# Key and query weights loaded behind the branch, layer 3's output read first, and unread products on TensorE

## The chip, the cores and the metric

The kernel runs on one core of one Trainium2 chip. The metric is the device time of one execution in microseconds, and the figure given is the median of several runs. The engines of a core work side by side, each through its own queue in order: TensorE (PE: matrix products, with a separate record for loading weights), VectorE (DVE), ScalarE (ACT) and GpSimd (POOL). SyncE (SP) issues the transfers between DRAM and on-chip memory; they run on 16 DMA engines.

## What is computed

Input x is 32 images of 1024 channels and 14 x 14 positions. Two residual layers follow one another, each behind a group normalisation:

```
x = x + conv(_gn(x))         # three convolutions as table look-ups
x = x + attention(_gn(x))    # linear attention
```

In the first layer each convolution is a softmax over 16 centroids for each group of inputs, multiplied by a table, with a batch normalisation over all images behind it; the third one's output is added to the layer's input. The second layer is

```
q = elu(Wq x[:, :512] + bq) + 1 ;  k = elu(Wk x[:, 512:] + bk) + 1
z = 1 / (q . mean(k) + 1e-6)
kv = rope(k) x^T / n ;  attn = (rope(q) kv) * z
out = attn + depthwise3x3(x)
```

for 16 heads of 64 channels. All is in float32.

## The kernel before, in words

`layers` runs the three convolutions over the images. Its last stage computes the third convolution in 14 chunks of 448 tokens: 8 products for each of 8 channel tiles (L1005), a copy out of PSUM on ACT (L1013), statistics on DVE (L1014), and one store of the chunk, 1792 KB, to the DRAM buffer `o3d` (L1022). `bn_final` then makes scale and bias of the batch normalisation (`sc3`, `bi3`, L325 to L329).

The exponentials are taken without subtracting a maximum; whether all sums stayed in range is collected in a small number, `again`. After `layers` stands a branch, `tc.If(again > 0)` (L1036), which runs everything once more in a slower, safe form if needed. With this data it is skipped. Every engine executes the jump. At the end of the branch SP waits on each of the semaphores of its eight outstanding DMAs, and the other engines wait for SP.

Eight tiles of 128 x 1024 values, `weights` (named `lut0` to `lut7`), hold the tables of the convolutions in turn and later the weights of keys (`wk`, the first four) and queries (`wq`, the last four). `attention_inputs` returns the pieces that prepare the attention while the convolutions still run: small tables, x of the first pair of images (`x1`, `x0`, by halves of the channels), and the second half of the third convolution's output for the first pair (`o3_0`, `o3_1`). Its function `projections` issues the eight loads of the weights, 512 KB each. Before the change it is called after `layers`, ahead of the branch (`weights4(None)`), and again in the branch (`repeated`), where the tables overwrite the tiles.

Behind the branch `tb = gn_b + bi3` is made on DVE (L1061), some borders are cleared on POOL, and then 16 pairs of images go through a plan. `do(engine, rank, weight, fn, reads, writes, ...)` enters a piece with its engine, a due time (`rank`, lower is earlier), an estimated duration, and the keys that it reads and writes. `Plan.write` then plays the pieces through with the estimates: whenever an engine is free it takes the ready piece of the lowest rank whose buffers (`Slot`, taken from rings of tiles) are to be had. The order so found is the order of the instructions in each engine's queue. What an instruction waits for on the chip follows from the tiles that it touches, not from the plan's keys.

For a pair p and a half h (h = 1 are channels 512 to 1023, from which the keys come, and it goes first), the pieces that matter here are:

- `load`: SP loads x (for p > 0) and two tiles `o` of 392 KB with the third convolution's output from `o3d` (L1172). The ring `o3q` for these has no tiles of its own; it gets `o3_0` and `o3_1` once the first pair's half h = 1 has read them. So the reads for half h = 0 of the first pair wait for DVE.
- `front`: for each of four channel tiles ACT scales x into PSUM (L1192), DVE adds `o` times `sc3` (L1201), adds x (L1206), and takes statistics (L1211).
- `group_norm`: PE averages over groups with a matrix `gavg` (L1233), DVE centres (L1241 to L1246), PE averages squares, DVE adds epsilon (`gve`, L1249), POOL makes scale and shift (`ga`, `gb`).
- `normalise`: ACT writes the normalised `y` (L1286) and the scaled `x` for the depthwise convolution's middle tap (L1286 too).
- `channels`: PE multiplies `y` by a column block of `wk` or `wq` (L1318, four products of 392 columns), ACT takes relu (L1327) and exp (L1330), DVE takes the maximum (L1335 or L1339).
- `rope`, `tokens`, `products`, `normalisers`, `attend`, `lepe`: rotation on POOL, transposes on PE with copies on ACT (L1380, L1383), products of keys and values (L1417), denominators, attention (L1522) and the depthwise taps on DVE (L1540).

PSUM has four tiles `mm` for these products, three `pa` and one `w`. The ring `qr` has five tiles of 128 x 784 values, for rotated queries.

## Time and profile before

| | us |
|---|---|
| three runs | 3863.39, 3867.28, 3868.2 |
| median | 3867.28 |
| the profiled execution | 3861.88 |
| its span, first to last instruction | 3860.0 |
| PE busy | 3715.2 |
| DVE busy | 3002.4 |
| POOL busy | 2300.7 |
| ACT busy | 1687.7 |

All times below are counted from the start of the span of the profiled execution. The convolutions take until about 2662 us, the last store of `o3d` is issued at 2661.92, the plan's first instruction runs at 2682.18, and the first key product starts at 2703.04. In the record of PE a product in float32 appears as two matrix products. "Busy" of PE is the time covered by products, and their ends are modelled; the granted clock (PEclk) is a share of the full clock. The instructions that wait, branch or issue a DMA stand under the engine's queue, such as SPq.

### The profile page before, as it was taken

Reading aid. Unit: us, or ns where it says so; the run is one execution under the profiler, and the core shown is the slowest. Engines: PE = TensorE matmul, PEld = TensorE weight load, DVE = VectorE, ACT = ScalarE, POOL = GpSimd, SP = SyncE. Lnnn points to the kernel's source line nnn. Section 1 sums busy time; section 2 is a strip of 40 time slices with the busy share of each in tenths; the row PEclk is TensorE's granted clock in tenths of the full one; section 3 lists DMA queues with packets and bytes.
Section 4 is the critical chain, followed back from the end, with each engine's and each line's share of the span. In section 5 each row is a group of like instructions: output and inputs, shape, how many; then the busy total and the mean of one; then the engine's idle time right before and its main releaser. Section 6 shows DMA issues by size and latency. Waiting matters only on the chain. (4 is left out here: it accounts for less than half of the span.)

```text
span 3860.0 us, 45872 instructions
## 1 busy us (share of the span) xinstructions
PE 3715.2 (96%) x16415; PEld 2079.6 (54%) x16415; DVE 3002.4 (78%) x4281; ACT 1687.7 (44%) x3851; POOL 2300.7 (60%) x1338
## 2 busy tenths in 40 slices
PE   8999999999999999999999999995999999999998
PEld 5555555554555545555444444442666666666665
DVE  8999999978888888888633333332699999999996
ACT  4555555533333323333221222111766776666664
POOL 7999999974444444444311111110887888878886
PEclk9999999999999999999999999997999999999999
DMA  3111100015343333333111111103123223222221
GB/s 116 34 35 34 34 25 26 17 54 125 71 85 79 76 74 81 81 74 70 44 47 38 38 38 38 38 20 124 36 78 89 78 84 91 82 82 84 82 80 34
DMA packets 219107, 243.16 MB, mean 63 GB/s; under 512 B 24368, under 2 KB 216752, under 8 KB 218872
## 3 DMA queue, kind: packets, MB, share of 16 engines
q1 hardware_dynamic: 218296, 240.02, 23.3%
q8 instruction: 131, 2.15, 0.2%
q14 instruction: 104, 0.85, 0.1%
q10 hardware_dynamic: 576, 0.15, 0.0%
HBM read 163.55 MB, written 76.56 MB: 62 GB/s over the span
## 5 line engine op out<-in xcount | busy, mean ns | idle before, releaser
L596 POOL TENSOR_TENSOR t<-t,r 128x1664 f32<-128x1664 f32 (+1 forms) x284 | 1063.9, 3746 | 1188.3 <-DVE r L595 1153.8
L640 PE MATMUL po<-t,lut 128*128 128x392 f32 x4096 | 1418.1, 500 | 0.5 <-POOL t L596 0.5
L640 PEld LDWEIGHTS po<-t,lut 128*128 128x128 f32 x4096 | 759.9, 190 | 626.7 <-issue 123.7
L558 ACT ACTIVATE t<-sc,cbias 128x392 f32<-128x392 f32 (+1 forms) x1136 | 578.9, 592 | 1032.1 <-PE sc L906 646.6
L1318 PE MATMUL mm<-y,lut 128*128 128x392 f32 x2048 | 721.7, 500 | 4.8 <-DVE q L1335 2.9
L1005 PE MATMUL po<-t,lut 128*128 128x448 f32 x1792 | 682.2, 541 | 1.7 <-issue 1.7
L570 DVE STREAM_TRANSPOSE tt<-t 128x1664 f32<-128x1664 f32 (+1 forms) x284 | 544.3, 1917 | 167.8 <-ACT t L558 167.8
L595 DVE STREAM_TRANSPOSE r<-rc 128x1664 f32<-128x1664 f32 (+1 forms) x284 | 546.6, 1925 | 21.3 <-DVE rc L589 0.9
L1540 DVE SCALAR_TENSOR_TENSOR pa<-y,lepe_w,pa 128x406 f32<-128x406 f32 x900 | 540.7, 636 | 17.9 <-PE pa L1522 15.1
L1005 PEld LDWEIGHTS po<-t,lut 128*128 128x128 f32 x1792 | 339.0, 190 | 341.7 <-issue 341.5
L1318 PEld LDWEIGHTS mm<-y,lut 128*128 128x128 f32 x2048 | 375.7, 191 | 257.6 <-issue 14.3
L1014 DVE BATCH_NORM_STATS2 stats<-o 128x6 f32<-128x448 f32 x112 | 68.9, 617 | 487.5 <-ACT o L1013 487.5
L587 DVE TENSOR_REDUCE sm<-tt 128x104 f32<-128x832 f32 (+2 forms) x284 | 423.0, 1490 | 5.4
L573 POOL TENSOR_TENSOR tt<-tt 128x832 f32<-128x832 f32 x128 | 247.4, 1933 | 7.8 <-DVE tt L570 7.8
L1013 ACT COPY o<-po 128x448 f32<-128x448 f32 x112 | 59.0, 527 | 425.6 <-PE po L1005 381.2
L589 DVE RECIPROCAL rc<-sm 128x104 f32<-128x104 f32 (+1 forms) x284 | 229.5, 808 | 9.8
L897 PE MATMUL sc<-patch,cw 64*128 64x392 f32 x1024 | 210.4, 519 | 4.6 <-ACT t L558 2.5
L597 ACT ACTIVATE sm<-sm 128x104 f32<-128x104 f32 (+1 forms) x284 | 86.0, 303 | 177.1 <-DVE rc L589 176.9
L1503 POOL TENSOR_TENSOR qr<-qr,zb 128x784 f32<-128x784 f32 x64 | 117.6, 1850 | 70.2 <-DMA zb<-zd 68.2
L897 PEld LDWEIGHTS sc<-patch,cw 64*128 64x128 f32 x1024 | 90.5, 186 | 115.8 <-issue 74.2
L1327 ACT ACTIVATE e<-mm,kbd 128x392 f32<-128x392 f32 x128 | 74.1, 579 | 170.4 <-PE mm L1318 168.4
L1192 ACT ACTIVATE w<-x,tb,gn_a 128x196 f32<-128x196 f32 x248 | 128.2, 517 | 44.2 <-DVE tb L1061 20.9
(175 smaller groups left out, 3975.6 us busy)
## 6 DMA issues: line engine op xcount, KB each, us to landing
patch<-h1d SPq DMA_DIRECT2D x248, 162.8 KB
x<-in_x_dram SPq DMA_DIRECT2D x32, 784.0 KB
o3d<-o SPq DMA_DIRECT2D x14, 1792.0 KB
x<-in_x_dram SPq DMA_DIRECT2D x64, 392.0 KB
o<-o3d SPq DMA_DIRECT2D x64, 392.0 KB
out_dram<-x SPq DMA_DIRECT2D x64, 392.0 KB
h1d<-pad SPq DMA_DIRECT2D x96, 225.0 KB
patch<-h1d SPq DMA_DIRECT2D x124, 108.5 KB
```

Source lines behind the costliest of these rows:

```text
L558: nc.scalar.activation(t[:, j, : sc.shape[1]], sc, AF.Identity if exact else AF.Exp, bias=bias[:, j : j + 1],)
L570: nc.vector.transpose(tt, tf)
L573: nc.gpsimd.tensor_tensor(tv[:, :, :8], tv[:, :, :8], tv[:, :, 8:], ALU.add)
L587: nc.vector.tensor_reduce(sm, tv, AX.X, ALU.add)
L589: nc.vector.reciprocal(rc, sm)
L595: nc.vector.transpose(r, bc(rc, 2, KC))
L596: nc.gpsimd.tensor_tensor(tf, tf, r, ALU.mult)
L640: nc.tensor.matmul(po[h], luts[b][:, j, h * P : (h + 1) * P], ts[u % len(ts)][:, j, :N2], start=(b == 0 and j == 0), stop=(b == 7 and j == 3),
L897: nc.tensor.matmul(sc, w8[r, 8 * h + 4 * (j // 2) + g], grid(pbuf[n % NPB][r, j // 2, g]), start=True, stop=False,)
L1005: nc.tensor.matmul(po, luts[g][:, m * P : (m + 1) * P], t3[h][:, g % 4, :], start=(g == 0), stop=(g == 7),)
L1318: nc.tensor.matmul(pv(), w[kt][:, m0 : m0 + P], ywin(p, first + kt), start=(kt == 0), stop=(kt == 3),)
L1540: nc.vector.scalar_tensor_tensor(acc, neighbours(p, c, offset(k)), lw[:, c, k : k + 1], acc, ALU.mult, ALU.add,)
```

## The change

Four edits.

The loads of the weights become eight separate functions, one for each tile. They are no longer called ahead of the branch, nor in it; the plan enters them on SP with ranks of -90 to -83, the key weights first, and each writes a key `("w", b)` that the products of keys or queries read. The branch has no load of the weights ahead of it any more.

The two reads of the third convolution's output for the first pair's half h = 0 go into two tiles of the ring `qr` instead of `o3q`, and get a rank of -99. So SP's queue after the branch begins with two reads of `o3d` into `qr`, four loads of `wk`, four of `wq`, and then x of the second pair; before, it began with x of three halves, and then the reads of `o3d`.

Two pieces of PE work are added, of 16 and of 10 products of the identity with `tb`, 256 columns each, with a rank of -50. Nobody reads their results. The second piece names the key of `gve` of the first half as one that it reads, so the plan puts it behind the second average of that half; the tiles that it touches do not make it wait for `gve` on the chip. In PE's queue 16 products come first, then the two averages of half h = 1, the ten products, the two averages of h = 0, and the first keys.

The plan is played through anew with these pieces, and its order in the later pairs comes out different in places; which instructions there are does not change.

```diff
-        def projections(_):
-            for b in range(8):
-                t = a["wkT" if b < 4 else "wqT"]
-                load_lut(b, t[(b % 4) * P : (b % 4 + 1) * P])
-
-        return [loads, third, tables], projections, [third, projections]
+        def projection(b):
+            t = a["wkT" if b < 4 else "wqT"]
+            return lambda: load_lut(b, t[(b % 4) * P : (b % 4 + 1) * P])
+
+        return [loads, third, tables], [projection(b) for b in range(8)], [third]
...
         again = layers(False, early)
-        weights4(None)
...
-                ot = Slot("o3q")
+                ot = Slot("qr" if p == 0 and h == 0 else "o3q")
...
-                    do(SP, rank - 11 + 8 * k, 0.45, third, (), [(ot, 0), (ot, 1)], lag=4.5)
+                    r = rank - 11 + 8 * k if p > 0 else -99
+                    do(SP, r, 0.45, third, (), [(ot, 0), (ot, 1)], lag=4.5)
...
+        def warm(n, need):
+            pw = Slot("mm")
+
+            def piece():
+                for _ in range(n):
+                    nc.tensor.matmul(
+                        pw()[:, : CT * B],
+                        ident,
+                        tb.rearrange("p c b -> p (c b)"),
+                        start=True,
+                        stop=True,
+                    )
+
+            do(PE, -50, 0.4 * n, piece, need, [pw])
...
             do(DVE, rank, 0.1, variance, [pv], [key("gve")])
+            if p == 0 and h == 1:
+
+                for n, need in ((16, []), (10, [key("gve")])):
+                    warm(n, need)
...
+            need = [("w", b) for b in (range(4) if keys else range(4, 8))]
+
...
-            do(PE, rank, 2.76, product, ys_ + done, [pq, *held], lag=0.25)
+            do(PE, rank, 2.76, product, ys_ + done + need, [pq, *held], lag=0.25)
...
+        for b in range(8):
+            do(SP, b - 90, 0.95, weights4[b], (), [("w", b)], lag=3.5 + b)
         for p in range(NP):
             pair(p, T * p)
```

## The prediction

> **What bounds the kernel now.** I read the page's busy slices first: TensorE (PE) is busy in nine tenths of nearly every slice, except one with 5 tenths and a granted clock of 0.7, the 28th, at about 2605 to 2702 us. That is where layer 3 of the convolution hands over to the attention plan. I then cut that stretch into windows (columns: length, busy time of each engine with its instruction count, granted PE clock, DMA share, GB/s).

> ```profile
> 2661.00:2664.00 3.00, 0.33 (x1) 0.00 (x0) 1.33 (x3) 0.53 (x1) 0.59 (x1) 0.97 0.30 112
> 2664.00:2668.00 4.00, 0.00 (x0) 0.00 (x0) 0.50 (x3) 0.00 (x0) 1.06 (x1) 0.50 1.03 342
> 2668.00:2672.00 4.00, 0.00 (x0) 0.00 (x0) 0.00 (x0) 0.00 (x0) 0.00 (x0) 0.50 1.01 353
> 2672.00:2679.00 7.00, 0.00 (x0) 0.00 (x0) 0.00 (x0) 0.00 (x0) 0.00 (x0) 0.50 1.02 412
> 2679.00:2682.00 3.00, 0.00 (x0) 0.00 (x0) 0.00 (x0) 0.00 (x0) 0.00 (x0) 0.50 0.08 29
> 2682.00:2690.00 8.00, 0.00 (x0) 0.00 (x0) 6.32 (x15) 6.77 (x14) 2.83 (x14) 0.50 0.87 264
> 2690.00:2703.00 13.00, 3.87 (x16) 3.62 (x17) 8.31 (x29) 5.81 (x13) 2.62 (x6) 0.50 0.45 147
> 2703.00:2708.00 5.00, 5.00 (x9) 2.79 (x10) 1.99 (x5) 2.47 (x6) 2.63 (x6) 0.50 0.01 2
> 2708.00:2733.00 25.00, 25.00 (x83) 14.58 (x83) 16.76 (x54) 24.26 (x54) 11.76 (x10) 1.00 0.17 48
> ```

> From 2666 to 2682 no engine computes and the DMA runs at 340 to 412 GB/s: a stall on transfers. From 2682 to 2703 DVE and ACT prepare the first pair and PE hardly works; from 2703 to 2708 PE works at half clock; after that it is full. The waits around the branch (engine, line, releaser: us, times, longest) and the branch's own instructions say which transfers:

> ```profile
> DVE tb L1061 <- SPq L1036: 16.5, 1, 16.5
> SPq L1036 <- SPq L1036: 10.8, 1, 10.8
> SPq L237 <- DMA o3d<-o: 1.2, 1, 1.2
> L1036 SPq COMPARE_BRANCH  x1: 50/50/50, 2670.5 to 2670.5; - x1
> L1036 DVEq COMPARE_BRANCH  x1: 72/72/72, 2665.5 to 2665.5; - x1
> L1036 DVEq EVENT_SEMAPHORE  x1: 21/21/21, 2672.5 to 2672.5; - x1
> ```

> SP reaches the branch at 2670.5, after issuing eight weight loads, and at its end waits for every DMA in flight until 2681.4; everybody else waits for SP. Lastly the timeline shows what follows:

> ```profile
> 2682.18 0.42 DVE L1061 TENSOR_TENSOR tb<-gn_b,bi 128x256 f32<-128x256 f32 x1 [16.53 <-SPq L1036]
> 2693.15 0.63 DVE L1201 SCALAR_TENSOR_TENSOR w<-o,sc,w 128x392 f32<-128x392 f32 x1 [2.49 <-DMA o<-o3d]
> 2696.02 0.17 DVE L1249 TENSOR_SCALAR gve<-mm 128x8 f32<-128x8 f32 x1
> 2698.22 3.64 ACT L1286 ACTIVATE y<-x,gb,ga 128x196 f32<-128x196 f32 x8 [1.61 <-POOL gb L1253]
> 2703.04 9.38 PE L1318 MATMUL mm<-y,lut 128*128 128x392 f32 x20
> 2708.50 0.59 ACT L1327 ACTIVATE e<-mm,kbd 128x392 f32<-128x392 f32 x1 [3.00 <-PE mm L1318]
> ```

> DVE stands 2.5 us for layer 3's output of the second half (o), with the first half's averages ready behind it. The first key products run at half clock and ACT waits 3.0 us for the first. From there to 3780 us PE never stops for long, so a microsecond won before 2703 is won at the end.

> [...] the clock changes here at 2612.61, 2616.02, 2663.81 and 2708.18, all whole multiples of 3.413 us apart. It also fell after a window that was 1.46 us busy of 3.4 (3035.9 to 3039.3), so a window need not be quite idle. [...] only 1792-byte packets (the store of o3d) until 2668, 4096-byte ones (weights) after it. [...] here DVE's jump over the branch took from 2665.5 to 2672.5 while two 8 KB instruction packets came in at 2668.6 and 2670.7 between data packets.

> **The change, part by part.** I count from the start of tb, which is the first work after the branch: 2682.18 now.

> *Loads behind the branch.* The last store of o3d is issued at 2661.92. The one before it, with no load behind it, was issued at 2608.25 and landed at 2614.74 (landing records): 6.5 us. So the last lands at 2668.4; from the last landing to tb takes 2682.18 - 2681.39 = 0.8 us: tb at 2669.2. That is one end. The other is DVE's jump: if its instructions come no sooner than now (2672.5), tb follows at about 2673.0. With no weight packets after 2668 the second instruction packet should come about 2 us sooner; I take 2670.5. Gain 11.7 us, between 9.2 and 13.0.

> *What the eight loads now collide with.* SP issues two reads of o3d, then eight loads, then x of pair 1, whose DMAs must wait for earlier ones on their semaphores. Data starts about 1.8 us after tb; 0.8 MB at 350 GB/s (x's rate) ends at +4.1, 2.1 MB of key weights at 412 at +9.3, the query weights at +14.4. The first keys come at +18.8 and the first query product five products later: 8 us and more of cover. x of pair 1 lands at about +17.5 where ACT wants it at +20.6, so 3 us of cover; its o3 at about +20, wanted at +21.6. Cost nothing; if the loads ran at half rate, the keys would still not wait, but x would come about 10 us late.

> *Layer 3's output first, into two qr slots.* It is on SP's queue ahead of everything and has a buffer of its own, so it lands at about +4.5, wanted at +7.8. DVE's 2.5 us stall goes. In DVE's new order one such operation (0.54) stands ahead of the last statistics: these end at +9.05 instead of +8.5.

> *Unread products.* 16 and then 10 products of the identity with tb, 256 columns. Nearest row, the same form with 196 columns at full clock:

> ```profile
> 17.81 4.81 PE L553 MATMUL sc<-x,ident 128*128 128x196 f32 x28
> ```

> Two records each, so 4.81/14 = 0.344 us; for 256 columns 0.449. Sixteen take 7.2 us at full clock, plus half the time in half clock. [...] I take +10.2. Behind them in PE's queue stands the first average, ready at +9.05: it loses 1.2 us. Then it takes 0.5 (as warm averages do at 2737) instead of 1.0. DVE's four small operations end at +11.5, the second average at +12.05, and gve, behind 1.3 us of DVE work, ends at +13.0 (now +14.0). The y's start 2.05 us after that (as now) and end at +18.7. The second ten wait for nothing in hardware; they follow the second average: 4.5 us, to +16.6, or to +18.3 if the clock fell for one window. DVE reaches the second half's statistics at +17.0; averages in between, keys at +18.75 (or +20.0), now at +20.86. The first product takes 2.7 us instead of 5.3: +21.4 (or +22.7). ACT comes to it after y, six x and two w, 3.9 us: +22.6. So ACT is late next, not PE: its first exponential goes from +26.3 to +22.6, gain 3.7. If the clock were low at the keys: 20.0 + 5.3 = 25.3, gain 1.0.

> *Order in the pairs.* The planner's order is the same up to the end of the first pair, then differs in places down to the last pair, whose closing 75 DVE instructions are again alike. Number and kind of instructions are the same. What it may cost is seen in PE's waits:

> ```profile
> PE mm L1380 <- ACT kt L1383: 23.3, 16, 2.5
> ```

> One wait of 1.5 us a pair, and four times a clock window lost behind it (1.7 us each). I take zero, and 5 us either way.

> **Sum.** 11.7 + 3.7 = 15.4, say 15 us. The profiled execution took 3861.9 (span 3860.0): 3847. The median shown is 3867.3, 5.4 above it, so 3852 against the median.

> **Rivals.** (a) The unread products miss: the clock falls in the thin window at +10 to +12, and the keys come late and cold. For it: a window 43% busy fell. Against: the ten follow at once. Gain 11.7 + 1.0 = 12.7: 3854.6. (b) The new order eats the gain: 15 pairs with 1 us more each, 3867. For it: PE is the bound in all of them, with only 2 us idle in 72. Against: the same mix and priorities. (c) Slower: the wait for ACT's copy of the key transposes doubles in 14 pairs (20.4 us), and with it the clock falls in all instead of four (10 x 1.7 = 17): 37.4 - 15.4 = +22, 3889. It decides from 1.1 us a pair on. For it: the wait exists in every pair and its window already fell four times. Against: PE's groups of like instructions are 651 instead of 654, so nothing is cut finer. (d) The branch does not end sooner, since DVE's jump is the bound at 2672.5 and later: 9.2 + 3.7 = 12.9, 3854.4.

> **Numbers.** Forecast 0.52, (a) 0.20, (d) 0.14, (b) 0.08, (c) 0.06. About 7.7 us, 0.2%, can be told from no change. Bounds of the sum without order: 10.2 to 17.7; with 5 us of order and 2.4 us of spread of the runs: 3843 to 3861. Faster 0.86, same 0.08, slower 0.06.

> **What would show it.** SP's wait at the branch shrinks from 10.8 us and tb starts at 2669 to 2673, no weight packets before it; DVE has no wait for o; the unread products fill PE from +0.5 to +10; the first key products take 2.7 us; PE's wait for the key transposes' copies stays near 23 us. It is wrong if tb starts after 2673, if keys wait for weights, or if PE's idle time in pairs 1 to 14 grows by over 8 us.

## The result, and the profile after

| | before | after |
|---|---|---|
| median, us | 3863.81 (3859.81 to 3868.2, 5 runs) | 3843.16 (3841.59 to 3844.58, 5 runs) |
| profiled execution, us | 3861.88 | 3843.16 |
| its span, us | 3860.0 | 3841.0 |
| mean granted PE clock | 0.985 | 0.990 |

The ratio is 0.9944, 95% interval 0.993 to 0.9959: faster by 20.6 us, where 15.4 had been forecast. (Two of the five runs of before came after the forecast.)

From the page of the kernel after, PE's busy tenths and the granted clock in 40 slices:

```profile
PE   8999999999999999999999999998999999999998
PEclk9999999999999999999999999999999999999999
```

The 28th slice had 5 tenths and clock 0.7; it has 8 and 0.9. The same stretch of the kernel after in windows (length, busy time of PE, PEld, DVE, ACT, POOL with instruction counts, granted clock, DMA share, GB/s):

```profile
2664.00:2668.00 4.00, 0.00 (x0) 0.00 (x0) 1.84 (x6) 0.20 (x1) 1.65 (x1) 0.74 0.67 246
2668.00:2672.00 4.00, 0.00 (x0) 0.00 (x0) 0.00 (x0) 0.00 (x0) 0.00 (x0) 0.50 0.61 223
2673.00:2679.00 6.00, 5.33 (x13) 4.30 (x14) 4.46 (x11) 5.21 (x11) 2.51 (x13) 0.50 0.83 257
2679.00:2683.00 4.00, 4.00 (x19) 3.50 (x18) 3.93 (x10) 2.08 (x5) 0.00 (x0) 0.92 1.02 411
2683.00:2691.00 8.00, 6.58 (x36) 5.61 (x34) 6.00 (x24) 3.51 (x9) 2.64 (x6) 1.00 1.05 394
2691.00:2696.00 5.00, 4.87 (x18) 3.03 (x19) 1.85 (x7) 4.97 (x12) 2.64 (x6) 1.00 1.10 340
```

DVE's idle time ahead of tb is 5.1 us long instead of 16.5, and the weights' 394 to 411 GB/s now lie under computing (2679 to 2691). The branch's own instructions in the kernel after (duration in ns, place in us):

```profile
L1034 SPq EVENT_SEMAPHORE  x8: 17/17/17, 2671.4 to 2671.9; - x8
L1034 SPq COMPARE_BRANCH  x1: 50/50/50, 2664.8 to 2664.8; - x1
L1034 DVEq COMPARE_BRANCH  x1: 72/72/72, 2667.8 to 2667.8; - x1
L1034 DVEq EVENT_SEMAPHORE  x1: 21/21/21, 2672.4 to 2672.4; - x1
```

SP reaches the branch at 2664.8 and is through with its waits at 2671.9. DVE's jump takes from 2667.8 to 2672.4, and the wait of tb names it. The timeline of the kernel after (start, us, engine, line, operation, idle time before it and its releaser):

```profile
2673.03 0.43 DVE L1059 TENSOR_TENSOR tb<-gn_b,bi 128x256 f32<-128x256 f32 x1 [5.07 <-DVEq L1034]
2673.67 10.08 PE L1223 MATMUL mm<-tb,ident 128*128 128x256 f32 x32 [10.04 <-DVE tb L1059]
2683.58 0.51 PE L1247 MATMUL mm<-gst,gavg 128*128 128x8 f32 x4
2685.34 4.56 PE L1223 MATMUL mm<-tb,ident 128*128 128x256 f32 x20
2688.01 3.64 ACT L1304 ACTIVATE y<-x,gb,ga 128x196 f32<-128x196 f32 x8 [4.45 <-POOL gb L1267]
2691.60 5.19 PE L1338 MATMUL mm<-y,lut 128*128 128x392 f32 x15
2695.19 0.56 ACT L1347 ACTIVATE e<-mm,kbd 128x392 f32<-128x392 f32 x1
```

No operation waits for o or for a weight, the averages follow the products at once, and ACT no longer waits for the first key product. With the last store at 2661.92 before and 2664.22 after, the two profiled executions compare so:

| part, us | before | after | gain | forecast |
|---|---|---|---|---|
| start to the last store | 2661.92 | 2664.22 | -2.30 | 0 |
| last store to tb | 20.26 | 8.81 | 11.45 | 11.7 |
| tb to the first exponential | 26.32 | 22.15 | 4.17 | 3.7 |
| first exponential to the end | 1151.54 | 1145.85 | 5.69 | 0 |

The head (the two middle rows) gave 15.6 us. The question for the experiments was the last row: whether the pairs really became quicker, and by what. The first row is not chance either, it seems: over all the kernels of this document, the last store came at 2661.92 to 2663.50 us in the four profiled executions with the loads ahead of the branch, and at 2663.74 to 2669.07 in the nine with the loads behind it, though the instructions of the convolutions are the same. Why is open.

### The profile page after: what moved, and what is told of

It reads as the page before. It is cut to its first block, busy times and chain, and to the rows that moved or that the text cites. A ratio compares the mean times of both kernels' runs of the same rounds, so it can differ in the third digit from the quotient of the medians.

```text
span 3841.0 us, 45969 instructions
## 1 busy us (share of the span) xinstructions
PE 3721.5 (97%) x16467; PEld 2085.5 (54%) x16467; DVE 3001.9 (78%) x4281; ACT 1688.2 (44%) x3851; POOL 2302.9 (60%) x1338
## 3 DMA queue, kind: packets, MB, share of 16 engines
q1 hardware_dynamic: 218296, 240.02, 23.4%
## 5 line engine op out<-in xcount | busy, mean ns | idle before, releaser
L1338 PEld LDWEIGHTS mm<-y,lut 128*128 128x128 f32 x2048 | 373.3, 189 | 253.5 <-issue 10.6
```

The lines of the kernel that those rows point to most:

```text
L1338: nc.tensor.matmul(pv(), w[kt][:, m0 : m0 + P], ywin(p, first + kt), start=(kt == 0), stop=(kt == 3),)
```

## The experiments

All medians below are from five rounds, with 5 to 21 runs each. Three groups of kernels were timed, the third on another chip, each beside the kernel before as it stands: it took 3849.41, 3848.75 and 3851.08 us there. So groups can be up to 2.3 us apart, and that kernel, unchanged, was some 14 us quicker than in its first five runs. The first group shows why that can be.

**1. The planner's order written out.** `Plan.write` goes over a Python set of five engine names, whose order can change from one run of Python to the next. That order decides ties: the plan lets only one engine at a time run a piece marked `port`, and DVE and POOL both have such pieces. I wrote it out in both kernels, in two ways:

```diff
-        engines = {p[0] for p in self.pieces}
+        engines = ("PE", "DVE", "ACT", "POOL", "SP")
```

These are before_d and after_d; before_p and after_p have `("PE", "POOL", "DVE", "ACT", "SP")`. With SP last, all 24 orders of the other four gave only two different orders of instructions of the kernel before, by whether DVE or POOL is asked first. In both profiled executions, before and after, the instructions of all engines stand as in the D order.

> The kernel before, with one line of the planner written out: its loop over the engines goes over a set of five names, whose order no one fixes; here it is PE, DVE, ACT, POOL, SP. This is the order that the profiled executions of before and after both show (ACT's and POOL's lines stand as in this kernel). Theory H (the change is worth what its head gains, and the rest of the 19 us is chance): about 3862, in line with the before profile. Theory L (the planner's loop is a lottery from build to build, and before and after drew different lots): this one is another lot than the median of before, and lies outside 3860 to 3868.

> The changed kernel with the same written-out order PE, DVE, ACT, POOL, SP. It differs from before_d only in the head and in the third layer's residual pieces of the first two pairs; all later pairs are instruction for instruction the same. Theory H: 15.6 below before_d (store to tb 11.45 and tb to first exponential 4.17, as the two profiles have it), so 14 to 17, and the time from the first exponential to the end agrees within 2 us with before_d's. Theory O (the changed order of the first pair or the changed loads make the pairs themselves quicker): 19 to 21 below before_d, with 5 to 6 us of it after the first exponential. Theory L: as H between these two, but the D and P kernels lie over 4 us apart.

> The kernel before with the planner's loop written out as PE, POOL, DVE, ACT, SP: POOL is asked before DVE[...]. From the first pair on the order of every engine is another than in before_d. Theory L: 4 us or more away from before_d in either direction, all of it after the first exponential. Theory H: within 2 us of before_d. Theory O: within 2 us of before_d as well.

> The changed kernel with PE, POOL, DVE, ACT, SP written out. Theory H: 14 to 17 below before_p. Theory O: 19 to 21 below before_p. Theory L: the time after the first exponential differs from after_d's by 4 us or more, while store to tb and tb to first exponential are the same as in after_d within 1 us.

| us | before | after | gain |
|---|---|---|---|
| D order, median | 3861.22 | 3843.58 | 17.6 |
| P order, median | 3849.62 | 3832.93 | 16.7 |
| D order, store to first exponential | 46.45 | 31.01 | 15.4 |
| P order, store to first exponential | 46.81 | 30.94 | 15.9 |

The lottery is real: the kernel before lies 11.6 us apart in its two orders, and the time of before in these groups is that of the P order (I have no trace of those runs, so that it drew P is inferred from the time). But the two kernels of the result had drawn the same lot, so it does not explain their last row. Like against like, the change brings 16.7 to 17.6 us, of which the head is 15.4 to 15.9; in D that is just above what theory H allowed and below what theory O wanted. These totals contain the later last store. In the profiled executions the stretch behind the first exponential became shorter by 8.5 us in D and 4.7 in P (5.7 in the result), and the last store came 1.3 and 4.7 us later (2.3 in the result). So the 2 us within which theory H saw that stretch agree were exceeded.

In D, before and after differ in order only in the first two pairs, besides the edits: 18 of POOL's 1338 instructions and 24 of ACT's 3851 stand elsewhere, none behind 2799 us. In P the change reorders nearly all pairs: over a hundred of POOL's instructions and some 300 of ACT's stand elsewhere, the last of POOL's at 3722 us.

Why P is quicker than D is seen in PE's waits from 2700 us on (engine, line, releaser: us, times, longest), first before_d, then before_p:

```profile
PE mm L1380 <- ACT kt L1383: 23.3, 16, 2.5
```

```profile
PE mm L1380 <- ACT kt L1383: 9.6, 9, 1.7
```

ACT's timeline in before_d shows what the copies stand behind:

```profile
3034.40 1.12 ACT L1569 ACTIVATE side<-y,lepe_w 128x392 f32<-128x392 f32 x2
3036.70 0.62 ACT L1569 ACTIVATE side<-y,lepe_w 128x392 f32<-128x392 f32 x1 [1.18 <-POOL x L1577]
3037.23 1.05 ACT L1192 ACTIVATE w<-x,tb,gn_a 128x196 f32<-128x196 f32 x2
3038.22 1.54 ACT L1383 COPY kt<-mm 105x512 f32<-105x512 f32 x3
```

PE waits for ACT's copy, ACT stands at `side` until POOL has added x, and the copy is behind it in ACT's queue. This one wait is 13.7 us shorter in P. From the first exponential to PE's last product all of PE's idle time is 32.7 us in before_d and 22.5 in before_p, and its time at half clock is 20.5 and 3.4, which is worth 7.8 us more (half of PE's busy time in it). Against these 18.0 us stand 5.2 us by which PE's busy time, counted at full clock, is longer in P; the stretch to the end is 12.8 us shorter.

**2. The head alone, and the order alone.** pin_p has the changed head and before_p's plan piece for piece; order_only_d has after_d's plan with the old loads and no unread products. In pin_p the head is written by hand ahead of the plan; the ten later products follow the instruction that writes `gve`, and the loads ahead of the branch are gone:

```diff
...
+            for k in range(2):
+                nc.sync.dma_start(tiles["qr"][3 + k], o3d[:, 2 * k : 2 * k + 2, :N2])
+            for b in range(8):
+                weights4[b]()
+            warm(16)
             plan.write()
```

> The head of the change alone on the order of before_p: the eight weight loads, the two first reads of layer 3's output (into two further tiles) and the 16 and 10 unread products are written by hand around the plan, and the plan is the one of before_p piece for piece, so every engine but SP has before_p's order from the first key on. Theory H (the gain is made in the head): 15.6 below before_p, 3834, at most 2 from after_p. Theory O (the planner's new order is part of the gain): 4 us or more above after_p, since the order is the old one. Store to tb 8.8 and tb to first exponential 22.2 in both theories.

> The complement: after_d's order and its first reads of layer 3's output, but the eight weight loads ahead of the branch as before, and no unread products. Theory H: store to tb back to 20.2; tb to the first exponential 24 to 26.3 (DVE's 2.5 us wait for o goes, the keys are still cold); total 0 to 3 below before_d, 3858 to 3861. Theory O: another 5 to 8 below that, 3851 to 3855, all of it after the first exponential.

pin_p took 3836.98 (3835.05 to 3841.82): 12.6 below before_p and 4.0 above after_p. In its profiled execution the first exponential comes at tb +23.24 instead of +22.13, and the clock was halved for one window from tb +20.2, at the keys: rival (a) of the prediction, in small. The head's 14.7 us in that execution is thus near the total, and theory H holds for the main part. The 4.0 us against after_p are twice what H allowed and lie at the border that O named. The first exponential accounts for 1.1 of them; the rest may be after_p's order of the pairs, which is another, or half-clock windows. order_only_d took 3860.37: 0.9 below before_d, though its head gains 2.7 (tb to first exponential 23.48). The new order and the early read alone are worth next to nothing in D, where little of the order is new; there theory O falls. In P it stays open. (The profiled execution, 3855.09, is the quickest of nine, 5.3 below the median.)

**3. The parts.** loads_pin_d is before_d with only the eight loads moved behind the branch, ahead of the plan. no_warm_d is after_d without the 26 unread products. The edit of loads_pin_d:

```diff
...
-        weights4(None)
...
+            for b in range(8):
+                weights4[b]()
             plan.write()
```

> before_d with one part of the change: the eight loads are issued behind the branch, ahead of the plan, and all else stays, so layer 3's output for pair 1's other half is read after them on SP's queue. Theory A (the parts add): store to tb 8.8, tb to first exponential 26.2, total 11.4 below before_d, 3850. Theory Q (the loads stand in front of that read): 4.2 MB at 412 GB/s are 10 us, so DVE's wait for o grows from 2.5 us to 9 to 13, the first exponential comes at tb +33 to +37, and the total is 0 to 5 below before_d, 3856 to 3861.

> after_d without the 26 unread products, all other instructions in after_d's order. Theory C (the products pay by the clock): the averages come 1.5 us earlier, the first exponential at tb +22 to +23 as before, but the key products then run at half clock[...], so 2 to 4 us above after_d, most of it after the first exponential. Theory N (the clock does not matter here, ACT and DVE set the pace): within 1 us of after_d. Theory B (they are in the way of the averages): 1 to 2 us below after_d.

loads_pin_d took 3860.95, 0.3 below before_d: nothing, as theory Q said. tb comes 8.83 us after the store, 11.4 sooner, but the first exponential comes at tb +35.15, 8.9 later. The timeline of loads_pin_d says who waits:

```profile
2674.09 0.43 DVE L1059 TENSOR_TENSOR tb<-gn_b,bi 128x256 f32<-128x256 f32 x1 [5.10 <-DVEq L1034]
2694.77 0.63 DVE L1199 SCALAR_TENSOR_TENSOR w<-o,sc,w 128x392 f32<-128x392 f32 x1 [12.20 <-DMA o<-o3d]
```

DVE's 2.5 us for o have become 12.2. So the early read of layer 3's output, which looked like a part worth 2.5 us, is what lets the moved loads pay at all.

no_warm_d took 3851.46 (3847.13 to 3856.36), 7.9 above after_d, twice and more what theory C gave the clock. The windows of no_warm_d from its first key product on:

```profile
2692.60:2697.70 5.10, 5.10 (x9) 2.86 (x10) 1.99 (x5) 2.83 (x7) 2.63 (x6) 0.50 0.90 273
2697.70:2703.00 5.30, 5.30 (x17) 3.00 (x16) 2.77 (x9) 4.91 (x11) 0.00 (x0) 1.00 0.08 9
```

The keys start at tb +18.67, as in after_d, and run 5.1 us at half clock: 2.6 us of PE's work lost. The loss is mostly not in the head: in the profiled executions the first exponential comes 1.9 us later than in after_d, the stretch behind it is 5.8 us longer, and the last store comes 1.4 us later, although the instructions of the pairs stand exactly as in after_d. That is again the unexplained row, now with the opposite sign.

**4. The pairs against the clock's windows.** I compared the 13 middle pairs, whose instructions are the same in all D kernels, in one profiled execution each, from the second to the fifteenth store of `zd` (a DRAM buffer for the values z of a pair; all pairs but the last store once). All figures are in us; "work" is PE's busy time less half of its time at half clock, and the last column is the whole execution less its kernel's median:

| | length | PE idle | at half clock | work | execution less median |
|---|---|---|---|---|---|
| before | 910.6 | 24.6 | 13.7 | 879.2 | -1.9 |
| before_d | 908.1 | 24.5 | 11.1 | 878.1 | +0.3 |
| loads_pin_d | 907.0 | 25.8 | 3.9 | 879.2 | +0.7 |
| no_warm_d | 904.2 | 23.2 | 5.2 | 878.5 | -2.3 |
| order_only_d | 902.6 | 23.4 | 0.9 | 878.8 | -5.3 |
| after | 900.9 | 21.6 | 3.5 | 877.5 | 0 |
| after_d | 897.6 | 19.8 | 0.2 | 877.7 | -4.5 |

The work is the same within 1.7 us; of the 13 us between the ends, 4.8 are PE's waits and 6.7 the half clock. The figures are of single executions: before and before_d have the same instructions in the same order, and so have after and after_d, and these lie 2.5 and 3.3 us apart. What stands ahead of a half-clock window is seen in two pairs with nearly the same wait. before_d, cut at the clock's own changes:

```profile
3032.74:3036.15 3.41, 3.41 (x63) 2.71 (x59) 3.41 (x7) 2.75 (x6) 3.41 (x3) 1.00 0.02 5
3036.15:3039.56 3.41, 1.48 (x14) 1.27 (x13) 3.38 (x4) 2.82 (x6) 3.41 (x5) 1.00 0.00 0
3039.56:3042.97 3.41, 3.41 (x14) 2.95 (x14) 3.41 (x9) 2.76 (x6) 0.99 (x2) 0.50 0.33 91
```

The same pair in after_d, cut at whole windows of its own clock:

```profile
3020.55:3023.96 3.41, 2.46 (x36) 1.83 (x28) 3.38 (x7) 2.16 (x6) 3.41 (x4) 1.00 0.00 0
3023.96:3027.37 3.41, 2.39 (x18) 2.23 (x19) 3.41 (x5) 3.41 (x8) 2.73 (x3) 1.00 0.05 20
3027.37:3030.79 3.42, 3.42 (x24) 2.27 (x24) 3.42 (x8) 3.03 (x7) 1.02 (x1) 1.00 0.56 171
```

PE waits 1.93 us for the copy of kt in the one and 1.97 in the other. In before_d the wait lies whole in one window, which is 1.48 us busy, and the next runs at half clock. In after_d a boundary cuts it in two, and the clock stays full. So a head of another length may also shift all later pairs against the windows, and cost or give a few us by that. To test it I shifted the head by the number of products in the first row:

```diff
-                for n, need in ((16, []), (10, [key("gve")])):
+                for n, need in ((12, []), (10, [key("gve")])):
```

w12_d and w12_p have 12, w20_d has 20; nothing else moves.

> after_d with 12 unread products instead of 16 in the first row; every other instruction stands in after_d's order. In after_d the first averages' statistics end at tb +8.9 and the averages start at tb +10.6, behind the products. Theory H: averages and first exponential 1.3 us earlier (tb +20.9), no clock lost, 1 to 2 us below after_d, 3842. Theory G (the pairs' place against the clock's windows counts as much as the head): the first exponential as in H, but the identical pairs behind it take another time than in after_d, 2 us or more in either direction.

> after_d with 20 products in the first row. Theory H: averages and first exponential 1.7 us later (tb +23.9), 1 to 2 us above after_d, 3845. Theory G: first exponential as in H, but the total does not follow it: it lies outside 0 to 3 us above after_d, since all pairs are shifted by 1.7 us of a 3.41 us window.

> after_p with 12 products in the first row, a version that may beat both kernels. Theory H: 1 to 2 us below after_p, 3831.5, first exponential at tb +20.9. Theory G: 2 us or more from after_p in either direction.

Averages and first exponential of w12_d in the timeline:

```profile
2672.53 0.42 DVE L1059 TENSOR_TENSOR tb<-gn_b,bi 128x256 f32<-128x256 f32 x1 [5.05 <-DVEq L1034]
2681.47 0.61 PE L1247 MATMUL mm<-gst,gavg 128*128 128x8 f32 x4
2693.38 0.57 ACT L1347 ACTIVATE e<-mm,kbd 128x392 f32<-128x392 f32 x1
```

The heads moved as computed: first exponential at tb +20.85 (12), +22.18 (16), +23.88 (20). The totals in D did not follow: 3845.12, 3843.58 and 3847.21, so 12 products are 1.5 us worse with a head 1.3 us better, and the 13 pairs took 902.6, 897.6 and 906.1 us in the profiled executions (half clock 7.5, 0.2 and 10.4). The groups ran on different chips, though, and the executions of w12_d, after_d and w20_d lie 2.9 and 4.5 below and 2.8 above their medians; as ratios to the kernel before beside them the totals are 0.9985, 0.9982 and 0.9989, with intervals that overlap. Theory G's sign is met in the traces, and the medians do not settle it. w12_p took 3831.56 (3829.75 to 3837.82), 1.4 below after_p as H said, which their runs cannot tell apart. It is the quickest kernel here: 11.6 us below the result above, and nearly all of that is the P order.

## Why the prediction was right in its mechanism and wrong in its size

- *Loads behind the branch*, 11.7 (9.2 to 13.0): 11.45. The place was that of rival (d): DVE's jump ended last, at 2672.4, 0.5 us after SP's waits. It did get shorter, 4.6 us instead of 7.0; in it 8 KB instruction packets came at 2670.2, 2670.5 and 2670.7, and that it waits for them was not shown, so 2670.5 for tb was an estimate. The last store came 2.3 us later, so the price of the forecast held, counted from the store.
- *What the loads collide with*, nothing: right. The key weights landed at tb +6.6 to +10.3 (forecast +9.3), the query weights at +11.6 to +15.4 (+14.4), x of pair 1 at +16.6 and +17.8 (+17.5), wanted at +20.3.
- *Layer 3's output first*: the wait went, as said. That this part is the condition of the first (12.2 us without it) was not seen.
- *Unread products*, averages at +10.2, keys at +18.75, exponential at +22.6: +10.55, +18.57 and +22.15. How long the products would run at half clock, and so the +10.2, was an estimate; it came to 5.9 us (2673.67 to 2679.61), beside 5.1 for the first keys before (2703.04 to 2708.18). The clock was full from tb +6.6 on, and rival (a) did not come.
- *Order in the pairs*, zero, 5 either way: 5.7 in the two profiled executions; 8.5 in D and 4.7 in P behind the first exponential, and 2.2 and 0.8 as totals less heads, where the later last store is in. The prediction said that the order "then differs in places down to the last pair". With the tie-break held fixed that holds in P alone; in D, and so in the two kernels of the result, it differs only in the first two pairs. What moved there was PE's waits and half-clock windows in an unchanged order: from the first exponential on, 20.5 us at half clock became 13.7 (before and after), or 10.2 (after_d).
- **The steps that failed** are terms of the sum. One is the last sentence of the sum: "The median shown is 3867.3, 5.4 above it, so 3852 against the median." That carried the difference between a profiled execution and a median of three runs over to another kernel. With the tie-break held, seven runs of before have the median 3861.22, beside a profiled 3861.54; the kernel after took 3843.16 in both. The second is the pairs' zero, and behind it the sentence "so a microsecond won before 2703 is won at the end": w12_d won 1.3 us in the head and none in its median, and no_warm_d lost 7.9 us in all where its keys lost 2.6. The third is the convolutions, put at nothing without a reason; the last store came 2.3 us later. The miss of 8.8 us is 5.4 from the first, 5.7 from the second and 0.2 from the head, less 2.3 from the third and 0.2 of rounding and edges. The bounds of the sum, 10.2 to 17.7, do not follow from its parts either, which give 10.2 to 16.7.
- Rivals (b) and (c), the pairs taking back the gain, did not come: PE's wait for the copies of kt is 23.3 us in before_d and 22.6 in after_d.

What stays open: how much of the gain in the pairs is the place of the pairs against the windows and how much chance, how much of it is order in P, and why the convolutions end later with the loads moved. One half-clock window is shown behind a window with 1.93 us of idle time; that the shift of the head decides it in the mean over many runs is not shown.

## What to carry to other kernels

Fix every tie-break of a planner before anything is compared: here an unordered set was worth 11.6 us, two thirds of the change under study. Here the eight loads moved behind the branch stood in front of the reads issued after them on the same queue (a wait of 2.5 us became 12.2), so what was wanted first had to be moved ahead of them in the same step. Compare a forecast with medians of one fixed order and of more than three runs, and do not lean on single profiled executions for differences of a few us: two here lay 4.5 and 5.3 us below their medians.

## What the runs showed of the hardware

```profile
2694.70:2698.12 3.42, 2.45 (x13) 1.83 (x13) 1.05 (x7) 3.42 (x8) 0.89 (x1) 1.00 1.11 334
2698.12:2701.53 3.41, 3.41 (x6) 1.66 (x5) 0.22 (x1) 2.32 (x6) 1.74 (x6) 0.50 0.92 312
```

In before and after, the stretches between two changes of the clock are 1 to 244 times 3.413 us. These windows do not start with the program: its first product stood 0.37, 3.33, 0.57, 1.85, 1.56 and 2.81 us ahead of a boundary in the executions of before, before_d, after, after_d, before_p and after_p. Yet the clock fell 1.67 to 1.89 us after the last store in all six, about 2660 us later, though the stores themselves lay 6.3 us apart. In before and before_d the pairs lost windows at the same places (3039.3 and 3039.6, 3319.2 and 3319.5). Why the windows lie alike there was not shown.
